# One natural tile fewer ahead, the bias row by products, rank counts two tiles earlier, and a new plan

## The chip, the cores and the metric

The kernel runs on one NeuronCore of a Trainium2 chip (the other cores are idle). The metric is the device time of one execution in microseconds. Each engine (TensorE, VectorE, ScalarE, GpSimd, SyncE) works through its own list of instructions in order; they wait for each other through semaphores. In the profile they are PE (with PEld for weight loads), ACT is ScalarE, DVE is VectorE, POOL is GpSimd and SP is SyncE, whose work here is to issue DMAs.

## The reference

Graph attention over 3327 nodes with 1024 features; the adjacency matrix is sparse (about 16 neighbours a row, the row itself among them):

```python
h = relu((x - mean(x)) / sqrt(var(x) + 1e-5))           # row by row
f, g = h @ Wf + bf, h @ Wg + bg
e = relu(f @ g.T)                                       # 3327 x 3327
attention = softmax(where(adj > 0, e, -9e15), axis=1)
out = x + attention @ (h @ W + bW)
```

## The kernel before

It never forms the 3327 x 3327 scores. With A = Wf Wg^T the score of a pair is q_i . h_j plus a number of row i, where q = h A + vb. The row vb = bf Wg^T has QW = 1026 columns like A and q: 1024, one that carries bg, and one of filling, so that three pieces of 342 columns (QB) make it up. A row's neighbours are gathered, dotted with q, and their softmax-weighted sum is multiplied by W once.

**Part 1** goes over the 26 natural tiles of 128 rows. Iteration i of its loop does, for tile i + 2, the row degrees on ScalarE (`degrees`, L714) and the keys on GpSimd (`keys`, L721: adjacency times column number), and for tile i the maxima of 16 segments on VectorE (`segments`, L790) and from them the list of neighbours (`listed`). SyncE loads adjacency tiles five ahead (`load_adj`, tile r), x tiles (xt), stores candidates (cd), lists (pd) and the normalised rows (hd). Beside it TensorE turns Wg block by block (`turned_g`, L873, then two copies by ScalarE, L874), turns Wf's blocks (`factor`), and makes A's 24 pieces (`product`, L893). The bias row is made by `bias` (L885): nine groups of products with one column each, one group behind each transpose of a block of Wg; `biases` copies them to vcol (L1042) and stores them with nine DMAs to a row in DRAM (vd, L1045), from which vb is loaded, spread over the partitions, in iteration 8. Tile WgT holds Wg turned; wT is a pool of two buffers for turned blocks of Wf (WfT) or of h.

The rows are then handled by falling degree. Ranks are counted: `one_hot` writes each row's degree as a one-hot row of 48 bins (tile oh, L813), TensorE multiplies those with triangular matrices (`before`, `after`, `several`, L821), and VectorE picks each row's count (`placed`). Since q of a tile needs A, and A is ready only late, some natural tiles have their q made in part 1 already: tiles 9, 11, 13, 15, 17 (AHEAD). `turn` turns their h, `third` makes a third of q (L925), and q is stored to qd. The 128 rows of highest degree among these five tiles' rows go to the general ranking, the others make EARLY = 4 tiles of their own; `ahead_ranks` (L841 to L853) finds their ranks, in iteration 20. A table of due times (BEGIN, SECOND, PERIOD) spreads the steps `product`, `factor`, `turn` and `third` over the iterations. What is left after the loop is done in calls of `go`, between the rest of the ranking; `found1` (L1253) turns ranks into the permutation perm, and own does so for the early tiles.

**Part 2** goes over 26 tiles of ranked rows (ORDER: the four early ones, then the rest by falling degree). CAPS gives the gathered rows a row of each tile needs. For each gathered row there is one gather by GpSimd (tile G, 26 buffers, L656) and one dot with q on VectorE (L1426); after the softmax (ScalarE, E; VectorE, `greatest`) each row but the first is added to the weighted sum, either on VectorE (L1479) or scaled on ScalarE (L1462) and added by TensorE while it is transposed (L1466). SHARE says how many go to TensorE. Then come the transposed sum, the product with W into PSUM tile p_o (L1494), which ScalarE has filled with bias first (L1482), the scaling (L1505), the addition of x and the scatter. A tile that isn't early has its h gathered and turned (L1406), and its own q made in three thirds (L1413) into tile p_q. The order of all this on the engines is written by a planner that runs when the kernel is built: `steps_of` lists the steps with costs and dependences, `planned` searches an order, and the instructions are recorded by planned start. `fresh` clears a PSUM bank.

## Time and profile before

| What | Value |
|---|---|
| median of 3 runs (lowest, highest) | 1283.0 us (1281.14, 1283.7) |
| profiled execution, its span | 1295.19 us, 1293.5 us |
| last VectorE operation of part 1; first dot of part 2 | 294.66 us; 309.56 us |
| TensorE busy | 1145.8 us (89%) |
| VectorE busy | 1132.5 us (88%) |
| GpSimd busy | 916.2 us (71%) |
| ScalarE busy | 616.8 us (48%) |
| DMA bytes, mean rate | 379.81 MB, 294 GB/s |

In a row of the time line stand the start, the length, the engine, the line, what is written from what, how many instructions were merged, and in brackets how long the engine had been idle and what ended that. In a row of groups stand the count, the busy time in all and the mean of one in ns, then the idle time before. A row of windows has the stretch, each engine's busy time, the clock granted to TensorE, the share of time that the DMA engines worked, and GB/s. TensorE's matmuls in 32-bit floats show as two records each.

### The profile page before, as it was taken

How to read it: one execution, taken by the hardware profiler on the slowest of the kernel's cores; microseconds unless marked ns; L12 is line 12 of the kernel's file. 1: busy time of each engine (PE TensorE's matmuls, PEld its weight loads, DVE VectorE, ACT ScalarE, POOL GpSimd, SP SyncE). 2: the span in 40 equal slices, each digit the busy share in tenths (PEclk: the TensorE clock that was granted, in tenths of full speed). 3: DMA queues.
4: the chain of work that ended last, by engine and by line, in shares of the span. 5: the costliest groups of instructions: out<-in, count | busy, mean ns of one | idle time of the engine just before them, and what ended most of it. 6: DMA issues, size and time to landing. Idle time of an engine off the chain costs nothing. (4 is left out here: it accounts for less than half of the span.)

```text
span 1293.5 us, 14849 instructions
## 1 busy us (share of the span) xinstructions
PE 1145.8 (89%) x4769; PEld 743.9 (58%) x4769; DVE 1132.5 (88%) x2196; ACT 616.8 (48%) x942; POOL 916.2 (71%) x683
## 2 busy tenths in 40 slices
PE   5979997877797729889999999999999989999997
PEld 5856664554565416565666656666566555555554
DVE  5339999984968998979999999999999899999993
ACT  3459898751465323563555442544344324332422
POOL 6469999606758757788777777676777767787731
PEclk9779999897899769889999999999999999999999
DMA  8369999867968977999999998898998979998852
GB/s 338 142 214 408 401 391 348 272 223 280 367 245 279 351 280 230 354 286 355 312 346 331 318 326 291 271 315 283 318 294 272 312 248 316 305 311 290 286 172 67
DMA packets 105170, 379.81 MB, mean 294 GB/s; under 512 B 16831, under 2 KB 20574, under 8 KB 101883
## 3 DMA queue, kind: packets, MB, share of 16 engines
q0 software_dynamic: 80160, 288.87, 66.3%
q1 hardware_dynamic: 24922, 89.90, 19.0%
q8 instruction: 39, 0.64, 0.2%
q14 instruction: 49, 0.40, 0.1%
HBM read 346.74 MB, written 31.99 MB: 293 GB/s over the span
## 5 line engine op out<-in xcount | busy, mean ns | idle before, releaser
L656 POOL DMA_INDIRECT G<-hd,ps x458 | 551.3, 1204 | 188.8 <-issue 102.4
L1426 DVE CUSTOM_DVE_ANT_0 junk<-G,q 128x1024 bf16<-128x1024 f32 x403 | 493.2, 1224 | 20.9 <-DMA G<-hd,ps 14.3
L1494 PE MATMUL p_o<-W_sb,yT 128*128 128x512 f32 x832 | 377.2, 608 | 48.3 <-ACT p_o L1482 27.5
L1479 DVE SCALAR_TENSOR_TENSOR G<-G,sc 128x1024 f32<-128x1024 f32 (+1 forms) x268 | 338.3, 1264 | 4.5 <-ACT G L1451 3.1
L1413 PE MATMUL p_q<-A_sb,hT 128*128 128x342 f32 x1056 | 321.8, 457 | 8.5 <-ACT p_q L1422 3.9
L1494 PEld LDWEIGHTS p_o<-W_sb,yT 128*128 128x128 f32 x832 | 159.0, 194 | 238.9 <-issue 183.7
L1413 PEld LDWEIGHTS p_q<-A_sb,hT 128*128 128x128 f32 x1056 | 198.8, 193 | 111.0 <-issue 14.6
L721 POOL TENSOR_TENSOR r<-r,iotaj 128x1664 f32<-128x1664 f32 (+3 forms) x50 | 184.4, 3742 | 55.5 <-ACT r L714 54.7
L1466 PE MATMUL p_y<-ident,G 128*128 128x128 f32 x1680 | 203.6, 277 | 22.6 <-ACT G L1462 12.9
L1466 PEld LDWEIGHTS p_y<-ident,G 128*128 128x128 f32 x1680 | 190.5, 143 | 49.4 <-ACT G L1462 18.1
L1462 ACT ACTIVATE G<-G,sc 128x1024 f32<-128x1024 f32 x184 | 195.9, 1137 | 0.1
L790 DVE MAX8 cand<-r 128x8 f32<-128x208 f32 (+2 forms) x416 | 118.6, 359 | 20.3 <-DMA cd<-cand 12.9
L893 PE MATMUL ps_A<-WgT,WfT 128*128 128x342 f32 x384 | 119.3, 470 | 0.0
L1426 DVE CUSTOM_DVE_ANT_0 junk<-G 128x1024 bf16<-128x1024 f32 x69 | 84.5, 1225 | 28.9 <-DMA G<-hd,ps 20.6
L1419 ACT COPY q<-p_q 128x342 f32<-128x342 f32 x66 | 29.1, 442 | 156.9 <-PE p_q L1413 77.9
L1505 ACT ACTIVATE xp<-p_o,rs 128x512 f32<-128x512 f32 x50 | 33.7, 682 | 136.8 <-PE p_o L1494 79.3
L893 PEld LDWEIGHTS ps_A<-WgT,WfT 128*128 128x128 f32 x384 | 74.8, 199 | 37.7 <-issue 4.8
L714 ACT ACTIVATE r<-r 128x3327 f32<-128x3327 int32 (+3 forms) x27 | 77.3, 2863 | 14.9 <-DMA r<-in_adj_dram 14.9
L1447 ACT ACTIVATE sc<-sc,nm 128x10 f32<-128x10 f32 (+10 forms) x36 | 11.0, 305 | 137.2 <-DVE nm L1437 93.7
L925 PE MATMUL ps_A<-A_sb,WfT 128*128 128x342 f32 x240 | 73.7, 465 | 0.0
L1490 ACT COPY yT<-p_y 128x512 f32<-128x512 f32 x52 | 30.1, 586 | 81.8 <-PE p_y L1466 73.7
L656 POOL DMA_INDIRECT xp<-in_x_dram,perm x25 | 47.0, 1881 | 20.5 <-ACT xp L1505 13.8
(177 smaller groups left out, 828.6 us busy)
## 6 DMA issues: line engine op xcount, KB each, us to landing
r<-in_adj_dram SPq DMA_DIRECT2D x24, 1663.5 KB, 12.4
xt<-in_x_dram SPq DMA_DIRECT2D x22, 512.0 KB, 13.1
hd<-xt SPq DMA_DIRECT2D x22, 512.0 KB, 11.0
G<-hd,ps POOLq DMA_INDIRECT x458
A_sb<-in_L_gnn_Wg_dram SPq DMA_DIRECT2D x8, 512.0 KB, 12.8
A_sb<-in_L_gnn_Wf_dram SPq DMA_DIRECT2D x8, 512.0 KB, 11.6
W_sb<-in_L_gnn_W_dram SPq DMA_DIRECT2D x8, 512.0 KB, 7.2
qd<-q SPq DMA_DIRECT2D x5, 512.5 KB, 7.4
```

The lines of the kernel that those rows point to most:

```text
L656: return nc.gpsimd.indirect_dma_start(out=to, out_offset=None, in_=table, in_offset=bass.IndirectOffsetOnAxis(ap=idx, axis=0), **kw,)
L714: nc.scalar.activation(r[:n, b:e], a[:n, b:e], AF.Sign, accum_out=to)
L721: eng.tensor_mul(r[:n, b:e], r[:n, b:e], iotaj[:n, b:e])
L790: nc.vector.max(cands[t][:n, s * 8 : s * 8 + 8], r[:n, s * SW : min(N, (s + 1) * SW)])
L893: nc.tensor.matmul(ps[:, :QB], WfTs[c][:, k, :], WgT[:, k, o : o + QB], start=(k == 0), stop=(k == KD - 1))
L925: nc.tensor.matmul(banks[t, i][:, :QB], hTs[t][:, k, :], A_sb[:, k, i * QB : (i + 1) * QB], start=False, stop=(k == KD - 1), skip_group_ch ...
L1413: nc.tensor.matmul(ps_q[(3 * t + i) % 2][:, :QB], hT[:, k, :], A_sb[:, k, i * QB : (i + 1) * QB], start=False, stop=(k == KD - 1), skip_gr ...
L1426: nc.vector.tensor_tensor_reduce(junk, row(t, k), q[:, :D], 1.0, 0.0, op0=ALU.mult, op1=ALU.add, accum_out=scs[t % 3][:, k : k + 1],)
L1462: nc.scalar.activation(g, g, AF.Copy, scale=scs[t % 3][:, k : k + 1])
L1466: nc.tensor.matmul(ps_y[g][:, c, :], of[:, (4 * g + c) * P : (4 * g + c + 1) * P], ident, is_transpose=True, start=((t, g) not in begun an ...
L1479: nc.vector.scalar_tensor_tensor(y, row_k, scs[t % 3][:, k : k + 1], y, op0=ALU.mult, op1=ALU.add)
L1494: nc.tensor.matmul(ps_o[o], yT[:, k, :], W_sb[:, k, o * CB : (o + 1) * CB], start=False, stop=(k == KD - 1), skip_group_check=True,)
```

## The change

Four natural tiles (11, 13, 15, 17) have their q made ahead instead of five, so three early tiles stand at the head of part 2 instead of four, and 23 tiles instead of 22 make their own q there. CAPS, ORDER and SHARE follow: 474 gathered rows instead of 472, 173 sums on TensorE instead of 184.

The bias row is made as three products like A's: `factor_b` writes bf into all 128 columns of a block, so that each of the three products gives a third of vb on every partition; ScalarE copies it to vb. The one-column products, vcol, vd, its nine stores and the load are gone. The first three pieces of A move from iterations 0 to 2 into iterations 3 and 4, and the steps behind them follow by a table of due times with new constants; from iteration 20 on it gives each iteration the same kinds of steps as before.

`ahead_ranks` is called in iteration 18, and the one-hot rows and counts that it needs come earlier too. The clearing of p_o's banks moves behind the first tile's q in part 2, and the planner makes its order from the new tables.

SyncE's queue at the start, before (r is an adjacency tile, A_sb holds rows of Wg or Wf, xt a tile of x, cd the candidates):

```order
L707 DMA A_sb<-in_L_gnn_Wg_dram 128x1024 x2
L707 DMA A_sb<-in_L_gnn_Wf_dram 128x1024
L697 DMA r<-in_adj_dram 128x3327 x2
L1045 DMA vd<-vcol 128x1 x8
L1046 DMA vd<-vcol 2x1
L697 DMA r<-in_adj_dram 128x3327
L707 DMA A_sb<-in_L_gnn_Wf_dram 128x1024
L767 DMA cd<-cand 128x128
L697 DMA r<-in_adj_dram 128x3327
```

And with the change:

```order
L706 DMA A_sb<-in_L_gnn_Wg_dram 128x1024 x2
L706 DMA A_sb<-in_L_gnn_Wf_dram 128x1024
L696 DMA r<-in_adj_dram 128x3327 x3
L766 DMA cd<-cand 128x128
L696 DMA r<-in_adj_dram 128x3327
L706 DMA A_sb<-in_L_gnn_Wf_dram 128x1024
```

The stores to vd no longer stand between adjacency tiles 5 and 6 (the last two rows of r before the stores are tiles 4 and 5). Wf's first block has moved behind Wg's last one (it stood behind Wg's third), and its second block behind adjacency tile 7.

TensorE behind the third transpose of Wg's blocks, before (ps_tr: transposes; ps_A<-bfT,WgT: one-column bias products; ps_A<-WgT,WfT: products of 342 columns):

```order
L885 MATMUL ps_A<-bfT,WgT 128x1 x8
L873 MATMUL ps_tr<-ident,A_sb 128x128 x8
L893 MATMUL ps_A<-WgT,WfT 128x342 x8
L873 MATMUL ps_tr<-ident,A_sb 128x128 x8
L885 MATMUL ps_A<-bfT,WgT 128x1 x8
L873 MATMUL ps_tr<-ident,A_sb 128x128 x8
L885 MATMUL ps_A<-bfT,WgT 128x1 x8
L873 MATMUL ps_tr<-ident,A_sb 128x128 x8
L885 MATMUL ps_A<-bfT,WgT 128x1 x8
L893 MATMUL ps_A<-WgT,WfT 128x342 x8
```

And with the change, from the first instruction to the first count:

```order
L872 MATMUL ps_tr<-ident,A_sb 128x128 x24
L888 MATMUL ps_A<-WgT,WfT 128x342 x8
L872 MATMUL ps_tr<-ident,A_sb 128x128 x24
L888 MATMUL ps_A<-WgT,WfT 128x342 x8
L872 MATMUL ps_tr<-ident,A_sb 128x128 x16
L888 MATMUL ps_A<-WgT,WfT 128x342 x8
L872 MATMUL ps_tr<-ident,A_sb 128x128 x8
L820 LDWEIGHTS tri
```

Wf's first block is turned behind all of Wg's blocks now, and the three products of 342 columns here are vb's, not A's.

TensorE at the head of part 2, before (p_t: h turned; p_q: q; p_y: sums transposed; p_o: product with W):

```order
L1347 MATMUL p_o<-ident 128x512
L1406 MATMUL p_t<-ident,G 128x128 x16
L1413 MATMUL p_q<-A_sb,hT 128x342 x24
L1528 MATMUL p_y<-one 1x1
L1413 MATMUL p_q<-A_sb,hT 128x342 x24
L1466 MATMUL p_y<-ident,G 128x128 x88
L1494 MATMUL p_o<-W_sb,yT 128x512 x16
```

And with the change:

```order
L1381 MATMUL p_t<-ident,G 128x128 x16
L1388 MATMUL p_q<-A_sb,hT 128x342 x24
L1323 LDWEIGHTS ident
L1323 MATMUL p_o<-ident 128x512
L1323 LDWEIGHTS ident
L1323 MATMUL p_o<-ident 128x512
L1505 MATMUL p_y<-one 1x1
L1388 MATMUL p_q<-A_sb,hT 128x342 x24
L1441 MATMUL p_y<-ident,G 128x128 x104
```

Both turn two tiles' h and make two q first; p_o's banks are cleared between the two q.

```diff
-CAPS = [37, 25, 23, 22, 21, 21, 20, 19, 19, 18, 18, 17, 17, 16, 16, 15, 15, 14, 14, 13, 12, 11, 21, 18, 16, 14]
-
-AHEAD = [9, 11, 13, 15, 17]
+CAPS = [38, 25, 23, 22, 21, 21, 20, 20, 19, 18, 18, 17, 17, 17, 16, 16, 15, 15, 14, 14, 13, 12, 11, 20, 17, 15]
+
+AHEAD = [11, 13, 15, 17]
...
-ORDER = [25, 24, 23, 22, *range(22)]
-SHARE = [10, 13, 13, 11, 18, 15, 13, 8, 10, 7, 5, 9, 6, 8, 4, 4, 8, 3, 0, 5, 2, 3, 1, 4, 0, 4]
+ORDER = [25, 24, 23, *range(23)]
+SHARE = [12, 14, 10, 18, 15, 11, 8, 10, 7, 5, 10, 6, 8, 4, 6, 7, 2, 2, 4, 0, 3, 3, 2, 3, 1, 2]
...
 LAG = 2
-BEGIN, SECOND, PERIOD = 40.0, 38.0, 7.5
+BEGIN, SECOND, PERIOD = 43.0, 17.0, 7.5
 
...
     n = len(ORDER)
-    add("PE", 0.1, 0.2, ("fm", 0), at=244.0)
+    add("PE", 1.0, 1.1, ("fm", 0), at=244.0)
     add("DVE", 0.15, 0.2, ("fl", 0), ("fm", 0))
...
     qd = dram.tile([NA * P, D + 1], FP, name="qd")
-    vd = dram.tile([QW], FP, name="vd")
 
...
             nc.vector.tensor_tensor_scan(incl, onesd, pre1[:, NA, :], 0.0, op0=ALU.mult, op1=ALU.add)
-            nc.vector.tensor_mul(wide5, mine, pre1[:, :NA, :])
-            nc.vector.tensor_reduce(sums2[:, 1, :], wide5, AX.X, ALU.add)
-            nc.vector.tensor_mul(wide5, mine, incl[:, None, :].to_broadcast([P, NA, NBIN]))
-            nc.vector.tensor_reduce(sums2[:, 0, :], wide5, AX.X, ALU.add)
+            nc.vector.tensor_mul(wide5[:, :NA], mine, pre1[:, :NA, :])
+            nc.vector.tensor_reduce(sums2[:, 1, :], wide5[:, :NA], AX.X, ALU.add)
+            nc.vector.tensor_mul(wide5[:, :NA], mine, incl[:, None, :].to_broadcast([P, NA, NBIN]))
+            nc.vector.tensor_reduce(sums2[:, 0, :], wide5[:, :NA], AX.X, ALU.add)
             nc.vector.tensor_tensor(r1, sums2[:, 1, :], sums2[:, 0, :], op=ALU.subtract)
...
 
-        def bias(c):
-            m = P if c < KD else QW - D
-            for k in range(KD):
-                nc.tensor.matmul(
-                    pv[:m, c : c + 1], WgT[:, k, c * P : c * P + m], bfT[:, k : k + 1], start=(c == k == 0),
-                    stop=(k == KD - 1), skip_group_check=True,
-                )
+        def factor_b():
+            WfTs[KD] = wT.tile([P, KD, P], FP, name="WfT")
+            nc.scalar.copy(WfTs[KD], bfT[:, :, None].to_broadcast([P, KD, P]))
 
...
                 )
-            emptied1.append(lambda: nc.scalar.copy(A_sb[:, c, o : o + QB], ps[:, :QB]))
+            to = A_sb[:, c, o : o + QB] if c < KD else vb[:, o : o + QB]
+            emptied1.append(lambda: nc.scalar.copy(to, ps[:, :QB]))
 
...
         plan = {i: [] for i in range(NT + 8)}
-        plan[2] = steps[3:4]
         at = BEGIN
-        for step in steps[4:]:
-            plan[max(3, int((at - SECOND) / PERIOD) + 3)].append(step)
+        for step in steps:
+            plan[int((at - SECOND) / PERIOD)].append(step)
             at += 1.1 if step[0] in (factor, turn) else 4.75
...
                 load_w(Wg, c)
-            transposed(WgT[:, :, :P], A_sb[:, 0, :D])
-            load_w(Wf, 0)
             load_adj(2)
...
 
-            pv = p_mm.tile([P, CB], FP, name="ps_A")
-
             def turned_g(cs):
                 for c in cs:
-                    if c:
-                        transposed(WgT[:, :, c * P : (c + 1) * P], A_sb[:, c, :D])
+                    transposed(WgT[:, :, c * P : (c + 1) * P], A_sb[:, c, :D])
                     empty()
-                    bias(c)
 
...
             keys(0, nc.vector)
-            empty()
-            bias(0)
+            factor_b()
+            turned_g((0,))
+            load_w(Wf, 0)
+            load_adj(4)
             degrees(1)
...
             turned_g((1, 2))
-            load_w(Wf, 1)
-            load_adj(4)
-            factor(0)
-            empty()
-
-            def biases():
-                bias(KD)
-                vcol = c1.tile([P, KD + 1], FP, name="vcol")
-                nc.scalar.copy(vcol[:, :KD], pv[:, :KD])
-                nc.scalar.copy(vcol[: QW - D, KD:], pv[: QW - D, KD : KD + 1])
-                for k in range(KD):
-                    nc.sync.dma_start(vd[k * P : (k + 1) * P, None], vcol[:, k : k + 1])
-                nc.sync.dma_start(vd[D:, None], vcol[: QW - D, KD:])
+            product(KD, 0)
 
...
 
-            placing = {i: i - 3 for i in range(3, 12)} | {12: 10, 14: 12, 15: 14, 18: 16, 19: 18, 20: 19, 21: 20, 22: 21}
+            placing = {i: i - 3 for i in range(3, 14)} | {14: 12, 15: 14, 17: 16, 19: 18, 20: 19, 21: 20, 22: 21}
             counted = None
...
                 if i < 2:
-                    product(0, i * QB)
                     turned_g(((3, 4, 5), (6, 7))[i])
+                    product(KD, (i + 1) * QB)
                 if i == 1:
-                    biases()
-                    factor(1)
-                if i == 8:
-                    nc.sync.dma_start(vb, vd[None, :].to_broadcast([P, QW]))
+                    factor(0)
                 empty()
                 fill_to(i + 1)
-                if i in (2, 6, 10, 14, 18):
+                if i in (2, 6, 10, 14):
                     one_hot(i - 2, i + 2)
-                elif i in (21, 22):
-                    one_hot(2 * i - 22, 2 * i - 20)
+                elif i in (16, 18, 20, 22):
+                    one_hot(i, i + 2)
                 if i in placing:
...
                     before(counted)
-                if i == 19:
+                if i == 17:
                     several(pre1, AHEAD)
-                if i == 21:
+                if i == 20:
                     for t in AHEAD:
...
                 for c in range(KD):
-                    if c > 1 and wants[c] - 2 == i:
+                    if c and wants[c] - 2 == i:
                         load_w(Wf, c)
...
                     placed(counted)
-                if i == 20:
+                if i == 18:
                     ahead_ranks()
...
             nc.scalar.copy(ps_q[i][:, :QB], vb[:, i * QB : (i + 1) * QB])
-            fresh(ps_o[i])
 
...
         def worst_of(_):
+            for ps in ps_o:
+                fresh(ps)
             nc.tensor.matmul(ps_y[1][0:1, 0, 0:1], worst, onesf, start=True, stop=True)
...
         def told(_):

```

## Prediction

> **What bounds the kernel now.** I read the busy time by stretches first, to split the program into stages, then each stage's own waits in order of time. Part 1 (ranks, normalised rows, weight product) ends at 294.66 us, when VectorE's last instruction of it releases the buffers; part 2 (gathers, dots, weighted sums, output product) fills the rest.
>
> The windows of part 1, columns PE, PEld, DVE, ACT, POOL, clock, DMA share, GB/s:
>
> ```profile
> 0.00:40.00 40.00, 25.13 (x114) 22.00 (x114) 16.79 (x52) 17.28 (x22) 23.76 (x58) 1.00 0.92 354
> 40.00:80.00 40.00, 38.75 (x178) 30.77 (x177) 13.62 (x54) 15.74 (x20) 19.13 (x6) 0.70 0.21 41
> ...
> 120.00:160.00 40.00, 38.60 (x157) 25.92 (x156) 38.94 (x160) 37.03 (x58) 40.00 (x12) 1.00 1.02 403
> ```
>
> From 120 us every engine is full: the loop over tiles runs at a steady pitch that nothing in the change makes shorter. From 40 to 80 us the DMA engines move 41 GB/s and VectorE works 13.62 of 40 us. The time line of SyncE's DMA issues says why:
>
> ```profile
> 24.60 1.65 SPq L697 DMA_DIRECT2D r<-in_adj_dram  x2
> 66.15 3.65 SPq L1045 DMA_DIRECT2D vd<-vcol  x8
> 74.37 0.36 SPq L697 DMA_DIRECT2D r<-in_adj_dram  x1
> ```
>
> The small stores of the bias row (eight, and a ninth) wait for the last bias column, and behind them in the same queue stand adjacency tile 6, whose buffer has long been free, and the first store of candidates, whose buffer tile 4 needs. Who waits for them:
>
> ```profile
> 71.48 14.66 POOL L721 TENSOR_TENSOR r<-r,iotaj 128x1664 f32<-128x1664 f32 x4 [12.56 <-ACT r L714]
> 86.08 2.98 ACT L714 ACTIVATE r<-r 128x3327 f32<-128x3327 int32 x1 [11.26 <-DMA r<-in_adj_dram]
> 87.54 4.52 DVE L790 MAX8 cand<-r 128x8 f32<-128x208 f32 x16 [12.91 <-DMA cd<-cand]
> ...
> 195.15 2.30 DVE L790 MAX8 cand<-r 128x8 f32<-128x208 f32 x8
> ...
> L714 ACT ACTIVATE r<-r 128x3327 f32<-128x3327 int32 (+3 forms) x27 | 77.3, 2863 | 14.9 <-DMA r<-in_adj_dram 14.9
> ```
>
> VectorE starts the maxima of tile 4 at 87.54 and of tile 18 at 195.15: (195.15 - 87.54)/14 = 7.69 us a tile. So whatever brings tile 4 forward brings all later tiles forward, as long as that pitch holds. The DMA engines are full at that pitch too (share 1.02), but they don't set it: of the 14.9 us that ScalarE waited for adjacency rows in the whole run, 11.26 lie at 86 us.
>
> Part 2, windows with the same columns:
>
> ```profile
> 400.00:500.00 100.00, 61.67 (x289) 39.98 (x288) 95.17 (x144) 33.94 (x45) 71.83 (x58) 0.80 0.85 303
> ...
> 600.00:800.00 200.00, 191.96 (x841) 124.77 (x840) 197.73 (x305) 96.82 (x152) 152.83 (x130) 0.99 0.94 324
> ...
> 1000.00:1200.00 200.00, 191.84 (x700) 114.43 (x699) 193.52 (x273) 66.88 (x114) 152.18 (x120) 0.99 0.89 296
> ```
>
> VectorE (99% and 97%) and TensorE (96%) are both the bound from 600 us on; before that TensorE has room.
>
> **The change part by part.** All sums are against the profiled execution (1295.19 us, span 1293.5, so 1.7 us around it). The runs shown have a median of 1283.0 us, 12 below; I carry the difference over unscaled, since 1% of it is nothing.
>
> *The bias row and the queue.* Removed are these products, the nine stores, the load of vb from DRAM, and the wait in SyncE's queue:
>
> ```profile
> L885 PE MATMUL ps_A<-bfT,WgT 128*128 128x1 f32 (+1 forms) x144 | 25.8, 310 | 0.5 <-ACT WgT L874 0.5
> ```
>
> Added are three products of 342 columns among Wg's transposes, one copy of 1024 columns on ScalarE (factor_b), and three copies into vb. Product (0,0) and the next ones start three tiles later. What now sets tile 4 is the chain of TensorE and ScalarE in front of its row of degrees, made of these pieces:
>
> ```profile
> 15.76 0.59 ACT L874 COPY WgT<-ps_tr 128x512 f32<-128x512 f32 x1 [6.16 <-PE ps_tr L873]
> 25.04 1.95 PE L873 MATMUL ps_tr<-ident,A_sb 128*128 128x128 f32 x8
> 27.02 0.59 ACT L874 COPY WgT<-ps_tr 128x512 f32<-128x512 f32 x1 [0.27 <-PE ps_tr L873]
> 37.70 1.03 PE L873 MATMUL ps_tr<-ident,A_sb 128*128 128x128 f32 x8
> 40.78 1.90 PE L873 MATMUL ps_tr<-ident,A_sb 128*128 128x128 f32 x8
> 51.15 6.50 PE L893 MATMUL ps_A<-WgT,WfT 128*128 128x342 f32 x16
> ...
> 74.21 4.85 PE L893 MATMUL ps_A<-WgT,WfT 128*128 128x342 f32 x16
> ```
>
> Step by step at the slow clock: block 0's copies end at 17.2 as now, and the degrees of tile 1 (2.98, the row at 86.08) at 20.2; blocks 1 and 2, no longer parted by bias products, are copied by 23.7; first bias product 6.5, to 30.3; blocks 3 to 5, each 1.95 with half of its copies hidden and 0.8 at the end, to 37.5; second product to 44; degrees of tile 3 (2.98 and 0.3 around it) to 47.3; block 6 copied 1.2, block 7 turned and copied 2.8, to 51.3; third product to 57.8; Wf's first block turned and copied, to 60.6; degrees of tile 4 to 63.9. GpSimd starts that tile's keys then instead of at 71.48, and its first half (14.66/4 = 3.7) lets VectorE in at 67.6. The later tiles follow GpSimd, 7.4 us each, until VectorE's own 7.69 is the longer, and their rows are early, since SyncE's queue now holds nothing that waits for TensorE. Gain 87.5 - 67.6 = 20. With every piece at its fast row (1.03, 4.85) the chain is 10 us shorter: gain 30. TensorE stops for ScalarE at several places of this chain, and the granted clock in 40 to 80 us was 0.70, so I take a value near the slow end, **21**. The early loads could cost something: the queue no longer stops at 16.6 us for Wf, so one more adjacency tile and a block of Wg (2.2 MB, 6 us at the 354 GB/s of the first 40 us) may be in flight when Wg's first block is awaited. Bounds 0 and 6; I take 0, since those loads stand behind it. The copy of bf hides in ScalarE's 6.16 us of idling before 15.76; without that cover it costs about 1.2 us, twice the 0.59 of 512 columns.
>
> The Trainium skill, in "TensorE: Matmul & The Clock Gate", section "Part 1: The HAM clock gate (the "warmup" mystery)", has it that the clock is released after some 3.4 us of sustained work and taken back after an idle window as long. By it the new chain, whose stops are shorter than 3.4 us but for the degrees of tile 3, would run warm almost throughout, which is the second of the two sums. The trace agrees only in part: right behind a product the transposes took 1.03, but 3 us later, with no such window between, they were back at 1.90.
>
> *The counts of ranks two tiles sooner.* They hold VectorE from 217.1 us until TensorE gets its next one-hot rows at 229, and most of that is not work:
>
> ```profile
> 217.09 0.25 DVE L841 TENSOR_TENSOR_SCAN incl<-onesd,pre 128x48 f32<-128x48 f32 x1
> ...
> 220.62 7.34 POOL L721 TENSOR_TENSOR r<-r,iotaj 128x1664 f32<-128x1664 f32 x2 [0.78 <-DVE sums L845]
> 220.80 3.55 DVE L847 TENSOR_SCALAR r<-r 128x5 f32<-128x5 f32 x1
> ...
> 228.02 0.17 DVE L849 TENSOR_SCALAR r<-r 128x5 f32<-128x5 f32 x1
> ...
> 229.33 0.20 PE L821 MATMUL pre<-oh,tri 128*128 128x48 bf16 x1 [11.45 <-DVE oh L813]
> ```
>
> A scalar operation on five columns takes 3.55 us while GpSimd multiplies a tile's keys, and 0.17 once it has stopped. At tile 18 GpSimd has keys to multiply too, so the 11.9 us move and don't go; four columns for five save nothing. What is late next is unchanged: ScalarE's scaling, then the next degrees. Bounds: 0, and -9 if GpSimd happened to stand still there; I take 0.
>
> *The tail of part 1.* From tile 22 on the order is the same, seven thirds of q included (one natural tile less is made, but the weight product runs three steps later). What differs is that TensorE comes out of the ranks' stall, slow, two tiles earlier:
>
> ```profile
> 202.56 9.45 PE L925 MATMUL ps_A<-A_sb,WfT 128*128 128x342 f32 x32
> 229.56 12.34 PE L925 MATMUL ps_A<-A_sb,WfT 128*128 128x342 f32 x32
> 274.17 0.18 DVE L1266 COPY tens<-pre 128x26 f32<-128x26 f32 x1 [3.15 <-PE pre L1253]
> 294.84 0.97 POOL L656 DMA_INDIRECT G<-hd,perm  x1 [15.31 <-DVE one L1342]
> 309.56 1.23 DVE L1426 CUSTOM_DVE_ANT_0 junk<-G 128x1024 bf16<-128x1024 f32 x1 [6.60 <-DMA G<-qd,own]
> ```
>
> The same 32 records took 2.9 us more, and later VectorE waited 3.15 us for the products behind them. Bounds 0 and 3; I take **2**. The hand-over (last VectorE operation, second gather, own q, first dot: 15 us) keeps its order, and the fillers of p_o that move behind the first q cost nothing there, because that q waits for the second gather anyhow.
>
> *Part 2.* One tile more makes its own q, and the plan moves weighted sums from TensorE to VectorE. CAPS grow from 472 to 474 gathered rows, SHARE falls from 184 to 173, so VectorE's sums (rows less 26 less SHARE) go from 262 to 275.
>
> ```profile
> L1426 DVE CUSTOM_DVE_ANT_0 junk<-G,q 128x1024 bf16<-128x1024 f32 x403 | 493.2, 1224 | 20.9 <-DMA G<-hd,ps 14.3
> L1479 DVE SCALAR_TENSOR_TENSOR G<-G,sc 128x1024 f32<-128x1024 f32 (+1 forms) x268 | 338.3, 1264 | 4.5 <-ACT G L1451 3.1
> L1413 PE MATMUL p_q<-A_sb,hT 128*128 128x342 f32 x1056 | 321.8, 457 | 8.5 <-ACT p_q L1422 3.9
> L1406 PE MATMUL p_t<-ident,G 128*128 128x128 f32 x176 | 28.0, 293 | 15.6 <-DMA G<-hd,perm 13.2 <-ACT hT L1409 2.4
> L1466 PE MATMUL p_y<-ident,G 128*128 128x128 f32 x1680 | 203.6, 277 | 22.6 <-ACT G L1462 12.9
> ```
>
> VectorE: 2 dots x 1.22 and 13 sums x 1.26 = +19. TensorE: a q of 321.8/22 = 14.6, its transposes 28.0/22 = 1.3, less 11 sums of 8 records (203.6/210 = 0.97): +5.2. Two more gathers on GpSimd and 11 fewer scalings on ScalarE lie beside that. With both engines full from 600 us the stage grows by something between 5 and 19: I take the middle, **+12**.
>
> Sum: -21 - 2 + 12 = -11. 1295.2 becomes 1284, the median 1283.0 becomes **1272**.
>
> **The rivals.** *Part 2 hides the extra q.* TensorE idles 38 of the 100 us at 400 to 500, and VectorE waits 35 us for gathered rows, nearly all before 600 (second row below); with one early tile less the large tile comes sooner. If these gaps take up 12 us, the stage stays as long: -23, 1260. Against it: VectorE, not TensorE, has the larger addition.
>
> ```profile
> 480.24 9.27 PE L1494 MATMUL p_o<-W_sb,yT 128*128 128x512 f32 x16 [21.96 <-ACT p_o L1482]
> ...
> DVE junk L1426 <- DMA G<-hd,ps: 34.9, 31, 7.9
> ```
>
> *Slower: ScalarE's order blocks the output products.* At 480.24 TensorE had waited 21.96 us for a filler of p_o that stands on ScalarE behind an exponential of the large tile. The plan is made anew from the same costs, so one more wait of this kind can come, with 38 rows in the large tile instead of 37. Then VectorE's 19 and these 22 are paid: -23 + 41 = +18, 1301. It decides from the point where part 2 grows by more than 23.
>
> *The warm chain.* The fast sum holds: -30 - 2 + 12 = -20, 1263.
>
> *The change doesn't do what it says.* The queue's gap closes, but tile 4 gains only what GpSimd gains (71.48 - 63.9 = 7.6), because something else in the early loop (Wg's loads that crowd, 6 us) takes its place: -7.6 - 2 + 12 = +2, 1285.
>
> **How the numbers follow.** Forecast 0.48, with its own range 1264 to 1280; hidden q 0.15; warm chain 0.12; blocked order 0.14; no gain in the loop 0.11. A change of 0.2% (2.6 us) is what a measurement of this kernel can tell. Faster: nearly all of the first three and a quarter of the last, 0.73; same 0.08; slower: the blocked order and part of the last, 0.19. The range for 8 in 10 runs from 1255, below the hidden q, to 1290, past the case without gain; the upper case at 1301 is left out with most of its chance.
>
> **What would show it.** Right: SyncE issues adjacency tile 6 before 40 us; tile 4's maxima start near 67 us and tile 18's near 175; three operations of 2 to 4 us stand in the ranks' counts; part 1's last VectorE operation lies near 272 and the first dot near 287; VectorE's busy time after that grows by 19. Wrong: DMA still slow in 40 to 80 us, a pitch above 7.7 us, or more than 23 us longer from the first dot to the end.

## The result: 5000.7 us, because the dense path runs after the fast one

The changed kernel takes 5000.73 us (median of 4 runs, 4996.6 to 5004.58) against 1283.02 before: 3.8985 times as long, 95% interval 3.8917 to 3.9052. The prediction was 1272, range 1255 to 1290. Runs more than 1.5% above the fastest of their kernel are left out of the medians and ratios here.

The kernel has two ways to the answer. `edge_path` gathers neighbours; when it has ended, `bad` is read, and with `bad > 0` the whole result is made once more by `dense_path`, which forms all scores. `bad` is the largest of three tests; the last one asks whether a row has more neighbours than CAPS allows its slot (slot: the place of a tile of ranked rows in CAPS). The changed kernel's most costly groups, and pieces of its chain of waits (start, length, what), show both paths, one behind the other:

```profile
L275 PE MATMUL acc<-xw,PT 128*128 128x512 f32 (+2 forms) x2704 | 1210.5, 607 | 174.4 <-DMA xw<-xw_d 174.4
L231 PE MATMUL ps_s<-T,fT 128*128 128x512 f32 (+3 forms) x2912 | 1174.7, 562 | 3.5 <-DMA fT<-fT_d 3.5
```

```profile
1254.12 8.08 DMA out_dram<-xp,final
1262.43 0.20 POOL ident masks.py:197
...
1267.46 12.82 DMA W_sb<-in_L_gnn_W_dram
...
1653.45 714.74 PE ps_fg L182 x1792
```

Neither ps_s nor acc occurs in the profile before. The fast path's last scatter starts at 1254.1 (1287.7 before), lands 8.1 us later, and right behind it the dense path makes its identity and loads W: 3.7 ms follow.

What the fast path did up to there answers the prediction's steps. The windows of its start, SyncE's issues, VectorE and the rest in the time line (rows as in the part on the profile before):

```profile
0.00:40.00 40.00, 21.33 (x88) 15.10 (x88) 16.79 (x52) 21.28 (x27) 27.01 (x58) 1.00 0.97 380
40.00:80.00 40.00, 33.67 (x133) 22.42 (x134) 33.20 (x131) 30.11 (x39) 33.06 (x9) 0.96 0.81 287
```

```profile
21.39 8.82 SPq L696 DMA_DIRECT2D r<-in_adj_dram  x3
30.26 0.42 SPq L766 DMA_DIRECT2D cd<-cand  x1
```

```profile
58.06 0.66 DVE L789 MAX8 cand<-r 128x8 f32<-128x208 f32 x2 [2.83 <-POOL r L720]
...
166.29 2.30 DVE L789 MAX8 cand<-r 128x8 f32<-128x208 f32 x8
...
173.11 0.34 DVE L841 TENSOR_TENSOR held<-oh,pre 128x192 f32<-128x192 bf16 x1
173.48 0.36 DVE L842 TENSOR_REDUCE sums<-held 128x4 f32<-128x192 f32 x1
173.87 13.12 DVE L843 TENSOR_TENSOR held<-oh,incl 128x192 f32<-128x192 bf16 x1
...
251.64 0.18 DVE L1242 COPY tens<-pre 128x26 f32<-128x26 f32 x1 [3.15 <-PE pre L1229]
...
272.01 0.16 DVE L1317 TENSOR_REDUCE one<-bads 128x1 f32<-128x3 f32 x1
...
287.72 1.23 DVE L1401 CUSTOM_DVE_ANT_0 junk<-G 128x1024 bf16<-128x1024 f32 x1 [6.50 <-DMA G<-qd,own]
```

SyncE's queue no longer waits for the bias row (it still waits up to 15.4 us at a time for VectorE to free an adjacency tile), the granted clock at 40 to 80 us is 0.96 (0.70 before), tile 4's maxima start at 58.06 (87.54), tile 18's at 166.29 (195.15), part 1 ends at 272.1 (294.66), the first dot starts at 287.72 (309.56).

### The profile page after: what moved, and what is told of

It is laid out like the page before. It is cut to its first block, busy times and chain, and to the rows that moved or that the text cites. A ratio compares the mean times of both kernels' runs of the same rounds, so it can differ in the third digit from the quotient of the medians.

```text
span 4994.8 us, 35657 instructions
## 1 busy us (share of the span) xinstructions
PE 4658.5 (93%) x13708; PEld 2377.4 (48%) x13708; DVE 1740.1 (35%) x3369; ACT 840.5 (17%) x1255; POOL 1062.6 (21%) x949
## 4 chain that ended last, share of the span: by engine, by line
PE 66%; DMA 6%; issue 4%; DVE 1%; POOL 0%; ACT 0%; POOLq 0%; DVEq 0%
PE ps_s L231 22%; PE acc L275 20%; PE ps_fg L182 14%; PE ps_xw L148 7%; DMA xw<-xw_d 6%; PE ps_t L251 1%; DVE G L1454 1%; PE p_o L1469 1%; PE ps_tr L136 0%; DMA W_sb<-in_L_gnn_W_dram 0%; DMA out_dram<-xp,final 0%; DVE junk L1401 0%; POOL W_sb L109 0%; DMA out_dram<-r 0%; DMA fT<-fT_d 0%
## 5 line engine op out<-in xcount | busy, mean ns | idle before, releaser
L275 PE MATMUL acc<-xw,PT 128*128 128x512 f32 (+2 forms) x2704 | 1210.5, 607 | 174.4 <-DMA xw<-xw_d 174.4
L231 PE MATMUL ps_s<-T,fT 128*128 128x512 f32 (+3 forms) x2912 | 1174.7, 562 | 3.5 <-DMA fT<-fT_d 3.5
L275 PEld LDWEIGHTS acc<-xw,PT 128*128 128x128 f32 (+2 forms) x2704 | 520.7, 195 | 814.0 <-issue 628.9
L231 PEld LDWEIGHTS ps_s<-T,fT 128*128 128x128 f32 (+1 forms) x2912 | 549.0, 190 | 595.9 <-issue 586.0
L235 DVE SCALAR_TENSOR_TENSOR S<-ps_s,lim 128x512 f32<-128x512 f32 (+2 forms) x182 | 118.9, 653 | 756.9 <-PE ps_s L231 756.9
L148 PE MATMUL ps_xw<-W_sb,T 128*128 128x512 f32 (+1 forms) x832 | 362.8, 593 | 3.9 <-DMA W_sb<-in_L_gnn_W_dram 3.9
L182 PE MATMUL ps_fg<-T,Wf_sb 128*128 128x512 f32 (+1 forms) x896 | 357.5, 562 | 0.8 <-DVE xw L155 0.8
L182 PE MATMUL ps_fg<-T,Wg_sb 128*128 128x512 f32 (+1 forms) x896 | 357.4, 561 | 0.0
L182 PEld LDWEIGHTS ps_fg<-T,Wf_sb 128*128 128x128 f32 x896 | 170.1, 190 | 188.6 <-issue 183.7
L182 PEld LDWEIGHTS ps_fg<-T,Wg_sb 128*128 128x128 f32 x896 | 170.1, 190 | 187.1 <-issue 183.7
```

What stands on the lines that cost most here:

```text
L148: nc.tensor.matmul(ps[:n], T[b][:, k, c0 : c0 + n], W_sb[:, k, o * CB : (o + 1) * CB], start=(k == 0), stop=(k == KD - 1),)
L182: nc.tensor.matmul(ps[:, :n], w_sb[:, k, d * P : (d + 1) * P], T[b][:, k, :], start=(k == 0), stop=(k == KD - 1),)
L231: nc.tensor.matmul(ps[:n, :w], fT[:, k, :n], T[b][:, k, :], start=(k == 0), stop=(k == KD - 1))
L235: nc.vector.scalar_tensor_tensor(sb, ps[:n, :w], 0.0, lim[:n, :w], op0=ALU.max, op1=ALU.min)
L275: nc.tensor.matmul(acc[t, o][:n], PT[:m, j, c0 : c0 + n], xw[:m, o * CB : (o + 1) * CB], start=(j == 0), stop=(j == NT - 1),)
```

## The experiments

Times are medians; a ratio is to the kernel before, run on the same chip in turns. Chips differ (before took 1280.9, 1284.3, 1314.8 and 1284.4 us in the four comparisons), so kernels are compared within one. Some of the edits are shown shortened. The repaired kernel is the changed one with the entry of CAPS put right, as described next.

### What sends the kernel into the dense path

The degrees follow from the inputs that the reference makes. With five tiles ahead, 1109 rows in the general ranking have 19 neighbours or more, and slot 9 begins behind 9 x 128 = 1152 rows, so 18 is enough for it. With four tiles ahead 128 more rows stand in that ranking, 1159 of them have 19 or more, and 7 of these fall into slot 9, whose entry in the new CAPS is 18. All other slots hold. So for this slot the new CAPS is one less than its rows need.

**The guard alone.** The test allows 19 in slot 9, while the plan still gathers 18: the 19th neighbour of the seven rows is left out, so this kernel serves to time only.

```diff
-                nc.gpsimd.memset(caps[:, j : j + 1], float(cap))
+                nc.gpsimd.memset(caps[:, j : j + 1], float(cap + (j == 9)))
```

> The guard alone is told that slot 9 holds 19 neighbours; the plan, the gathers and every order stay those of the changed kernel, so in slot 9 the 19th neighbour of the rows that have one is left out. By the degrees of the inputs 7 of the 128 rows in slot 9 have 19 neighbours against a cap of 18, and no other slot is exceeded. Theory (only that one entry of CAPS sends the kernel into its dense path): the dense rows vanish and the time is that of the fast path as its trace shows it: last scatter at 1254.1 us against 1287.7 before, so 1295.2 - 33.6 = 1261.6 for a profiled execution and about 1250 for the median. Rival A (another test of the guard trips too, the count of the lists or a degree below one): 5000 as before. Rival B (the fast path takes what I predicted, because the trace of the long execution is not that of a short one): 1272.

Measured: 1262.6 us against 1280.9, ratio 0.988 (0.981 to 0.995); the dense rows are gone. One entry of a test is the whole of the 3.7 ms.

**The entry itself**, with which every slot holds what its rows need:

```diff
-CAPS = [38, 25, 23, 22, 21, 21, 20, 20, 19, 18, 18, 17, ...
+CAPS = [38, 25, 23, 22, 21, 21, 20, 20, 19, 19, 18, 17, ...
```

> CAPS[9] is 19 instead of 18, in the tables and so in the plan, which is made anew with one more gathered row, 475. Theory: the fast path alone, as in the run with the guard changed, plus one dot and one sum on VectorE (1.22 + 1.26 = 2.5 us): 1252 median. Rival (the search finds another order, and its luck is worth more than the row): anything between 1240 and 1265, with the waits of TensorE for fillers on ScalarE (22 us in one piece before, 18.9 in one piece after) appearing or going. By the predicted sum it would be 1274.

Measured: 1260.9 against 1280.9, ratio 0.985 (0.983 to 0.988). This is the repaired kernel. Both lie 9 to 13 us above what I expected, because I had carried a difference of two profiled executions over to medians: the profiled execution of the guard's run took 1260.1, where 1261.6 was expected (see the base, below).

**The same fault in the kernel before.**

```diff
-CAPS = [37, 25, 23, 22, 21, 21, 20, 19, 19, 18, 18, 17, ...
+CAPS = [37, 25, 23, 22, 21, 21, 20, 19, 19, 17, 18, 17, ...
```

> The kernel before with one entry of CAPS one too small (slot 9: 17 instead of 18, where all 128 rows have 18 neighbours). Theory (one slot too small is enough, whatever else the kernel does): the fast path runs to its end and the dense path after it, as in the changed kernel: 1283 + (5000.7 - 1250) = about 5034 us. Rival (the changed kernel falls back for a reason of its own, in the counts or the ranks): 1281, one row less than before.

Measured: 5018.9 us in one run. From the last scatter to the end it is 3737 us, in the changed kernel 3741: one entry that is one too small costs the same in either.

### The start of the loop: queue or chain

**The nine stores later**, in the kernel before:

```diff
                 if i == 1:
-                    biases()            # copies to vcol, and nine stores
+                    vcol = biases()     # copies only
+                if i == 5:
+                    stored_biases(vcol) # the nine stores
```

> The kernel before, with the nine small stores of the bias row issued in iteration 5 instead of iteration 1, where they wait for nothing; products, copies and TensorE's order stay. It tells SyncE's queue from TensorE's chain in the 21 us that the start of the loop was forecast to gain. Theory: GpSimd's keys of tile 4 stay at 71.5 us, since they wait for ScalarE and TensorE, and VectorE starts on tile 4 a quarter of that later, near 75 instead of 87.5: 12 us gained, 1271. Rival A (the queue is all of it): tile 4 near 67, 20 us gained, 1263. Rival B (the stores only show TensorE's lateness, and the row of the loop is bound by TensorE's weight product, which is not moved): no gain, 1283.

Measured: 1287.7 against 1280.9, ratio 1.005 (1.003 to 1.008): slower by half a per cent. SyncE's issues and VectorE's wait behind them:

```profile
84.69 14.72 SPq L1048 DMA_DIRECT2D vd<-vcol  x8
99.46 0.34 SPq L1049 DMA_DIRECT2D vd<-vcol  x1
```

```profile
76.21 2.31 DVE L790 MAX8 cand<-r 128x8 f32<-128x208 f32 x8 [1.87 <-POOL r L721]
...
116.54 1.29 DVE L730 BATCH_NORM_STATS2 st<-xt 128x6 f32<-128x512 f32 x2 [11.77 <-DMA xt<-in_x_dram]
```

Tile 4 came forward by 11.3 us as the theory said, but issuing eight stores of 128 single numbers took 14.72 us here, where they had taken 3.65 in the idle stretch before; 9.9 of it the profile puts down to waits for earlier transfers (candidates, an adjacency tile, x). The loads behind them were late and VectorE waited 11.77 us for x. Rival B's number is the nearest, but not its reason: tile 4 did gain, and the gap only moved.

**The bias row turned, and stored by two DMAs**, in the kernel before:

```diff
-                for k in range(KD): nc.sync.dma_start(vd[k * P : (k + 1) * P, None], vcol[:, k : k + 1])
-                nc.sync.dma_start(vd[D:, None], vcol[: QW - D, KD:])
+            # iteration 2: one transpose of vcol, one copy to vrow; iteration 4:
+                    nc.sync.dma_start(vd[:D].rearrange("(k p) -> k p", p=P), vrow[:KD, :])
+                    nc.sync.dma_start(vd[None, D:], vrow[KD:, : QW - D])
```

> The kernel before, with its bias products, but the row is turned once (one transposition, one copy) and stored by two DMAs of whole rows in iteration 4, instead of nine of single numbers. Moving the nine stores to iteration 5 brought tile 4 forward by 11.3 us (76.21 against 87.54), but their issue then held SyncE for 14.72 us with the other queues full (3.65 before), and the gain was lost. Theory (the queue is worth what tile 4 gains, as long as nothing else blocks SyncE): tile 4 near 76, pitch 7.7, part 1 to 283, median 1270. Rival (what tile 4 gains is lost again later in the loop, at the loads of x or the weight product): tile 18 at 190 or later, 1278 to 1283.

Measured: 1277.3 against 1284.3, ratio 0.994 (0.991 to 0.997). Tile 4's maxima come at 75.6 us, part 1 ends at 286.8: of the 12 us some 8 arrive at the end of part 1. The 1270 of the theory was too low: by the table below tile 18 is still 11.4 us sooner, tile 22 only 7.6, and between them lie the ranks, whose stall grew (see the counts of ranks, below). Closing the gap in the queue alone is worth about 7.

**The old bias row in the repaired kernel**: `bias` behind each transposed block, `biases` with its nine stores and the load in iteration 8 are back, `factor_b` and `product(KD, ...)` are gone.

> The changed kernel with CAPS[9] = 19 and the bias row as before: one-column products behind each transposed block, nine stores, a load in iteration 8. Theory (the forecast's term of 21, all of it in the bias row): tile 4's maxima near 87 again, part 1 to 289, median 1282. Rival (part of the 21 comes from the weight product's start two iterations later, which stays here): tile 4 near 78, part 1 near 280, median 1272.

Measured: 1278.5 against 1284.3, ratio 0.995 (0.992 to 0.997); the repaired kernel with late ranks stood beside it at 0.981. So the bias row is worth 18.4 us of the gain, 1278.5 - 1260.1, or some 16 if the late ranks of that kernel are worth the 2.5 us that the direct comparison below leaves open. The other 6 (1284.3 - 1278.5) are still there with the old bias row. Each expectation was half right: tile 4's maxima start at 76.2, as the rival had it, and part 1 ends at 289.0, as the theory had it. The start of VectorE's list of tile 4 (its first operation after the maxima) and of later tiles, from each kernel's time line, with the ends of the stages:

| | tile 4 | tile 18 | tile 22 | part 1 ends | last scatter |
|---|---|---|---|---|---|
| before | 92.1 | 199.8 | 242.1 | 294.7 | 1287.7 |
| turned bias row | 81.6 | 188.4 | 234.5 | 286.8 | 1269.7 |
| old bias row, else repaired | 80.7 | 190.5 | 233.0 | 289.0 | 1272.9 |
| changed | 64.1 | 170.9 | 217.2 | 272.0 | 1254.1 |
| repaired (direct comparison below) | 62.3 | 169.1 | 215.3 | 269.9 | 1251.8 |

### The terms on one chip

For three terms the spread between chips was larger than the term, so four kernels ran side by side in five rounds.

**Five tiles ahead** (the new start and the sooner counts stay; AHEAD, CAPS, ORDER and SHARE are before's). First run, then the direct comparison:

> The changed kernel with five tiles ahead as before: the tables CAPS, AHEAD, ORDER and SHARE of before, so part 2 is planned from before's tables; the new start of the loop and the sooner counts stay. TensorE has one more q, 15 us, to make in the tail of part 1. By the forecast's terms (21 gained at the start, part 2 the 12 shorter that a fourth early tile is worth): 1249 if the tail hides the q, 1264 if it hides nothing. By what the traces say now (part 2 takes 966 to 971 us with before's plan in two other profiles, and 964 to 967 with the new one, so nothing is lost by four): 1261 if the tail hides the q and 1276 if it hides nothing.

> The changed kernel with CAPS[9] = 19, as the base of a direct comparison on one chip: 0.98 to 0.985 of the kernel before.

> Five tiles ahead with before's tables, new start of the loop, sooner counts. By the forecast's term (part 2 is 12 us longer with four): 12 us below the base less what its tail pays (part 1 ended 1 to 5 us later in the traces): 7 to 11 below. By the traces (part 2 as long with either): 1 to 5 above.

Measured first: 1265.3 against 1284.3 (0.983, 0.980 to 0.987). Side by side: repaired 1262.0, five ahead 1263.9, before 1284.4 (both ratios 0.983, 0.981 to 0.986). Four tiles or five make no difference that can be measured. The part from the end of part 1 to the last scatter, as one window each, repaired and five ahead:

```profile
270.00:1253.00 983.00, 903.88 (x3708) 567.30 (x3708) 927.40 (x1403) 408.33 (x631) 712.29 (x580) 0.96 0.87 297
```

```profile
271.00:1257.00 986.00, 899.52 (x3759) 570.41 (x3757) 908.99 (x1375) 417.89 (x633) 705.61 (x577) 0.96 0.87 296
```

VectorE works 18.4 us longer with three early tiles instead of four and TensorE 4.4, but VectorE is idle for 983.0 - 927.4 = 55.6 us instead of 986.0 - 909.0 = 77.0. The extra work goes into the gaps. Two thirds of the difference in idle time lie ahead of 600 us, as the windows of the same two kernels up to there show:

```profile
270.00:600.00 330.00, 275.68 (x1282) 186.90 (x1283) 299.71 (x484) 154.10 (x217) 243.88 (x214) 0.90 0.90 324
```

```profile
271.00:600.00 329.00, 264.71 (x1280) 182.98 (x1279) 283.97 (x461) 155.93 (x214) 242.50 (x207) 0.90 0.91 319
```

**Counts of ranks two tiles later**, in the repaired kernel:

```diff
-            placing = {...} | {14: 12, 15: 14, 17: 16, 19: 18, ...}
+            placing = {...} | {14: 12, 15: 14, 18: 16, 19: 18, ...}
-                if i == 17: several(pre1, AHEAD)      if i == 18: ahead_ranks()
+                if i == 19: several(pre1, AHEAD)      if i == 20: ahead_ranks()
```

> The changed kernel with CAPS[9] = 19 and the counts of ranks two tiles later again, as before (one-hot rows, counts, the placing of tile 16 and the ranks of the tiles ahead). Theory (the forecast's term of 0: the stall moves with them): within 2.6 us of 1261. Rival A (sooner counts are worth something, since the stall no longer lies next to the tail, where TensorE has the weight product and q to make): 1264 to 1268. Rival B (they cost, since the stall has grown from 11.9 to 15.7 us in the changed kernel's trace, one product of 192 columns taking 13.1 us beside GpSimd): 1257.

> The counts of ranks two tiles later, four tiles ahead. Its trace ended part 1 at 266.9, the base's at 268.0 on another chip, with the same 16.5 us for the stall. If the stall only moves: within 2.6 us of the base. If sooner counts gain or cost: further away than that, to one side.

Measured first: 1260.1 (0.981, 0.978 to 0.984). Side by side: 1259.5 against 1262.0 for the repaired kernel, ratios 0.981 (0.978 to 0.983) and 0.983. Sooner counts gain nothing; whether they cost the 2.5 us, the intervals leave open.

**The ranks' operands in PSUM.** The stall in the ranks was 16 us in the changed kernel, not 12: one product takes 13.12 us (row above), whose two inputs, oh and incl, are both in SBUF. In this kernel no operation of VectorE in the ranks reads two operands from SBUF:

```diff
-            nc.vector.tensor_tensor_scan(incl, onesd, pre1[:, NA, :], ...)
+            nc.vector.tensor_tensor_scan(incl_p, onesd, pre1[:, NA, :], ...)   # incl_p lies in PSUM
-            nc.vector.tensor_mul(wide5[:, :NA], mine, incl[:, None, :]...)
+            nc.vector.tensor_mul(wide5[:, :NA], mine, incl_p[:, None, :]...)
     # likewise sums2[:, 1], r1 and a second copy of top: views of a PSUM bank
```

> The changed kernel with CAPS[9] = 19, and in the ranks of the tiles ahead every operation of VectorE takes at most one operand from SBUF, the other from PSUM (the running count, the differences and the marks lie there). In the run with CAPS[9] = 19 the one product whose two inputs are both in SBUF took 13.04 us, from 172.41 to 185.45, and GpSimd's unbroken run of keys ended at 185.22; the product before it, of the same shape and with one input in PSUM, took 0.34. Theory (VectorE waits for GpSimd only where both operands come from SBUF, and the wait is as long as GpSimd has keys in hand): no operation of the ranks above 1 us, part 1's end 12 to 13 earlier (255), median 1249. Rival A (something else is late then, ScalarE's degrees or TensorE's counts): 1257 to 1261. Rival B (any operation but the maxima waits for GpSimd): the 13 us stand at another operation, 1261.

> The kernel with CAPS[9] = 19 once more, to stand beside the others of this comparison: 0.985 of the kernel before, as before.

> The same with the operands of the ranks in PSUM. Its trace showed the 13 us wait gone and part 1 ended 11.1 us sooner than in the run beside it, but the first dot only 5.9 sooner, and the medians, 10.3 apart, came with wide intervals. If the first dot's 6 us count: 0.5% below the base. If part 2 takes them back: the same. If part 1's whole 11 count: 0.9% below.

Measured first, on the chip with the longest times: 1278.0 against 1284.8 for the repaired kernel and 1314.8 before (ratios to before 0.971, 0.963 to 0.979, and 0.978, 0.970 to 0.987). Side by side: **1252.3** against 1262.0, ratio 0.975 (0.973 to 0.977) to the kernel before: 32 us faster than before, and the best version of this study. GpSimd's run of keys and the ranks, first in the repaired kernel, then in this one:

```profile
137.06 47.79 POOL L720 TENSOR_TENSOR r<-r,iotaj 128x1663 f32<-128x1663 f32 x13
...
171.34 0.34 DVE L841 TENSOR_TENSOR held<-oh,pre 128x192 f32<-128x192 bf16 x1
171.72 0.36 DVE L842 TENSOR_REDUCE sums<-held 128x4 f32<-128x192 f32 x1
172.11 12.97 DVE L843 TENSOR_TENSOR held<-oh,incl 128x192 f32<-128x192 bf16 x1
185.11 0.36 DVE L844 TENSOR_REDUCE sums<-held 128x4 f32<-128x192 f32 x1
```

```profile
138.74 55.20 POOL L720 TENSOR_TENSOR r<-r,iotaj 128x1663 f32<-128x1663 f32 x15
...
173.40 0.36 DVE L841 TENSOR_TENSOR held<-oh,pre 128x192 f32<-128x192 bf16 x1
173.80 0.37 DVE L842 TENSOR_REDUCE pre<-held 128x4 f32<-128x192 f32 x1
174.20 0.36 DVE L843 TENSOR_TENSOR held<-oh,held 128x192 f32<-128x192 bf16 x1
174.59 0.36 DVE L844 TENSOR_REDUCE most<-held 128x4 f32<-128x192 f32 x1
```

GpSimd's run ends at 137.06 + 47.79 = 184.85, and the waiting product at 185.08. With one operand in PSUM it takes 0.36 in the middle of such a run. Part 1 ends at 261.0 instead of 269.9, the first dot starts 9.1 us earlier, and the median follows by 9.7: this wait is on the path that sets the end.

### The planner's luck

The seed of the planner's search changed, in the kernel before and in the repaired one:

```diff
-SEED = 1
+SEED = 2        # in the kernel before; 6 in the repaired one
```

> The kernel before with another seed of its planner: same steps, another order found. It tells whether the lengths of part 2 (966 to 978 us from first dot to last scatter with before's tables, 964 to 967 with the new ones) come from the tables or from the order that the search happens on. Tables: within 3 us of the kernel before. Order: 5 us or more away from it, to either side.

> The changed kernel with CAPS[9] = 19 and another seed of its planner. Tables: within 3 us of the same kernel with seed 1 (1261), with VectorE idle for some 40 us in part 2 again, against 59 to 71 with before's tables. Order: 5 us or more away.

Measured: before with seed 2 takes 1327.8 against 1314.8 (1.012, 1.007 to 1.017); the repaired kernel with seed 6 takes 1282.5 against 1284.8 with seed 1, whose intervals overlap. Another order from the same tables can cost about 1%, 13 us here. A difference of that size between two plans can't be put down to their tables.

## Why the prediction was wrong, step by step

**The step that failed.** "CAPS grow from 472 to 474 gathered rows" took the table as a cost and didn't ask whether it still holds what it has to. The rival that the change doesn't do what it says looked at the loop alone. A fallback was nowhere in the rivals, though the test and the branch are in the kernel and the degrees follow from the inputs. The profile of before could not show it: there the branch is never taken, and none of its instructions is in any view. What the runs showed in its place: seven rows of slot 9 have 19 neighbours where the entry is 18, the test trips, and the dense path adds 3.74 ms. The range missed by 3.7 ms for this reason only: the repaired kernel's 1260.9 and 1262.0 lie inside it, near its lower end, since the terms below were off as well.

**The start of the loop, -21: right in mechanism, too small.** Tile 4's maxima came 29.5 us earlier, not 20, and SyncE issued adjacency tile 6 by 30 us as forecast. The same chain stood in front of it, but most of its pieces took the shorter of the two times that before's rows had shown, and I had taken the longer:

```profile
28.96 1.03 PE L872 MATMUL ps_tr<-ident,A_sb 128*128 128x128 f32 x8
30.24 1.14 PE L872 MATMUL ps_tr<-ident,A_sb 128*128 128x128 f32 x8 [0.24 <-ACT WgT L873]
31.58 1.15 PE L872 MATMUL ps_tr<-ident,A_sb 128*128 128x128 f32 x8 [0.19 <-ACT WgT L873]
32.91 4.87 PE L888 MATMUL ps_A<-WgT,WfT 128*128 128x342 f32 x16 [0.19 <-ACT WgT L873]
...
43.18 6.53 PE L888 MATMUL ps_A<-WgT,WfT 128*128 128x342 f32 x16 [0.28 <-ACT WgT L873]
```

These are rows behind the first bias product: 1.03 to 1.15 for a block, not 1.95, and 4.87 for the second product. The first (6.90) and the third stayed near the 6.5. The warm chain was a rival at 0.12 with a gain of 30. Here the rule of the Trainium skill that the prediction weighed, in "TensorE: Matmul & The Clock Gate", section "Part 1: The HAM clock gate (the "warmup" mystery)", agrees with the trace but for the third product: the clock granted in 40 to 80 us was 0.96, and fell to 0.50 only at 44 to 46 us, behind a stop of 3.10 us beside the degrees of tile 3. I gave the one row at 1.90 more weight than it deserved. It stood among one-column products, of which the new chain has none. In the kernel with the old bias row they are back, and TensorE is busy without a stop from 14.45 to 58.4 us:

```profile
14.45 1.94 PE L873 MATMUL ps_tr<-ident,A_sb 128*128 128x128 f32 x8 [14.45 <-DMA A_sb<-in_L_gnn_Wg_dram]
16.22 3.58 PE L885 MATMUL ps_A<-bfT,WgT 128*128 128x1 f32 x16
...
56.65 1.97 PE L873 MATMUL ps_tr<-ident,A_sb 128*128 128x128 f32 x8
```

Every block takes 1.94 to 1.97 there. So the old bias row not only held SyncE's queue, it also went with long transposes, and 44 us of work of this kind made them no faster: the rule as the prediction told it, released by some 3.4 us of sustained work, doesn't hold for such work. The pitch held nearly: (166.29 - 58.06)/14 = 7.73, not 7.69.

**The counts of ranks, 0: the place moved for nothing, but the stall grew.** "The 11.9 us move and don't go" held only for their kind. From the scan to the next maxima it is 172.96 to 188.97, 16.0 us against 12.1 before (217.09 to 229.19), and one operation of 13.12 instead of three of 2 to 4. The stall is no constant: the product waits as long as GpSimd's run of keys goes on. The trace of before has the same wait, at the 2.00 us of the first of the three:

```profile
205.07 14.77 POOL L721 TENSOR_TENSOR r<-r,iotaj 128x1664 f32<-128x1664 f32 x4 [0.33 <-ACT r L714]
```

```profile
218.12 2.00 DVE L844 TENSOR_TENSOR held<-oh,incl 128x240 f32<-128x240 bf16 x1
```

GpSimd's run ends at 219.84 and the product at 220.12; that the run was nearly over made it short. The late counts in the direct comparison and the turned bias row show the growth too (20.2 us between the lists of tiles 20 and 21 before, 23.6 and 24.0 in those). In the kernel with the old bias row, where the counts come sooner and SyncE's queue still stops, the same step (tiles 18 and 19) takes 20.1, in the changed kernel 24.0. So the growth comes with the closed queue gap, not with the new place. That rows which arrive earlier give GpSimd more keys in hand fits this, but wasn't tested by itself.

**The tail, -2: not there.** From tile 18's maxima to the end of part 1 the changed kernel takes 105.8 us, before 99.5: 3.9 of the 6.3 are the stall, 2.4 stay. The wait of 3.15 us for the products behind the ranks is unchanged. So part 1's end, forecast near 272 and measured at 272.1, came out right by luck, since a start that gained too much was eaten up by the stall and the tail: 29.5 - 0.6 (the pitch) - 3.9 - 2.4 = 22.6, next to the forecast's 21 + 2.

**Part 2, +12: its work was right, its length wrong.** The work grew by 18.4 us on VectorE and 4.4 on TensorE, where 19 and 5.2 were forecast (21 on VectorE with the repaired kernel's one more row, at the same prices); the length, on one chip and in one execution each, went from 985.4 us (part 1's end to last scatter, five ahead) to 981.9. "With both engines full from 600 us the stage grows by something between 5 and 19" was the wrong step: of VectorE's 77.0 us without work, 45 lay ahead of 600 us with five ahead, of the 55.6 with four 30, and these gaps and later ones took the work up, as the rival "Part 2 hides the extra q" said at 0.15, with -23 and 1260. Its mechanism is the one that fits the repaired kernel: 1262.0 against 1284.4 is -22.4. That the number fits as well is in part luck, since its start and tail were the forecast's. Which part is due to the tables and which to the order found stays open, since the seed alone moves about 1%.

**Slower, ScalarE's order.** The wait of this kind did come again, at another place. In the waits of the changed kernel's part 2 (us in total, times, longest) the 21.96 us for a filler of p_o is gone, and TensorE waits for fillers of p_q:

```profile
PE p_q L1388 <- ACT p_q L1397: 27.6, 6, 18.9
```

What it cost by itself isn't shown; the fast path ended 33.6 us sooner than before's all the same.

**The base.** The profiled execution of before was 12 us above the median, and I carried that over unscaled as if it were spread. It was not only that: from part 1's end to the last scatter it took 993.1 us, while five other profiles of before's tables and seed (one of them with one row fewer) took 982 to 991 there. Gaps of part 2 read from that one execution were partly its own: its longest wait for a gathered row was 7.9 us, in the five others 3.6 to 5.5.

## What to carry to other kernels

Where a kernel has a guard and a fallback, a table that feeds the guard is a condition before it is a cost: work out from the inputs whether each entry holds, for it decides about a factor of four, not about two rows. A stall that comes from another engine's run is not a constant that moves with its step; ask how long that run will be after the change. And work added to an engine that is 97% busy in one stretch can vanish in the gaps of other stretches, as the 18 us of VectorE did here.

## What the runs showed of the hardware

- A product on VectorE with both inputs in SBUF ended 0.2 to 0.3 us behind the end of GpSimd's unbroken run of keys, after 12.97 us in the repaired kernel, more than three of GpSimd's instructions of 3.7 us, and after 2.00 in the kernel before. The same product with one input in PSUM took 0.36 beside GpSimd. The Trainium skill, "SBUF — State Buffer", section "Who interferes with whom", says that two SBUF inputs contend with a GpSimd instruction that reads SBUF, and that at most one SBUF input, outside VectorE's 2-port modes, does not: the trace agrees. It gives the lock's length as one instruction, in its section "SBUF: two separate sides", and here the wait lasted over several. In the kernel with the old bias row two products of four columns, both inputs in SBUF, took 3.62 and 3.63 us, one GpSimd instruction each; what lets a product in between two instructions stays open.
- Issuing eight DMAs of 128 single numbers took SyncE 3.65 us with idle queues and 14.72 us in the full loop, 9.9 of them waits for earlier transfers.
- In the kernel with the old bias row the profile gives the granted clock as 1.00 from 14 to 60 us, while every block of transposes takes 1.94 to 1.97 us, against 1.03 to 1.15 at 28.96 to 32.7 us in the changed kernel, where the clock reads 1.00 too. So in such a stretch the granted clock alone doesn't tell how long a block takes.
- One of the chips took 1314.8 us for the kernel before, against 1281 to 1284 on the others.
